# A two-layer centroid convolution block: patch transfers one per slot, the norm six slots earlier, an image's last steps split between ScalarE and VectorE

## The chip, the cores and the metric

The kernel runs on one core of one Trainium2 chip. The metric is the device time of one execution in microseconds; the time before is a median of three runs. A core has TensorE (PE in the profile; its weight loads are PEld), VectorE (DVE), ScalarE (ACT), GpSimd (POOL) and SyncE (SP). Each engine works through its own instructions in the order written and waits on semaphores for the others. Transfers are issued from the queues of ScalarE, GpSimd and SyncE.

## The reference, cut to what matters

The block works on 16 images of 256 channels and 28 x 28 pixels. It is `x + relu(SE(BN2(amm2(relu(BN1(amm1(gn(x))))))) + gn(x))`, where `gn` is a group norm with 32 groups, SE a squeeze-and-excite gate, and `amm` a 3 x 3 convolution replaced by soft look-ups:

```python
patches = jax.lax.conv_general_dilated_patches(x, (3, 3), (stride, stride), 'SAME')
p = patches.reshape(B, C, s, Ho * Wo).transpose(0, 3, 1, 2)
d = jnp.sum(p * p, axis=-1)[..., None] - 2.0 * jnp.einsum('bncs,cks->bnck', p, centroids) + ...
attn = jax.nn.softmax(-d, axis=-1)
lut = jnp.einsum('cks,cso->cko', centroids, w_sub)
out = jnp.einsum('bnck,cko->bno', attn, lut)
```

For each pixel and channel the nine neighbours are compared with 16 centroids, the softmax over them mixes the centroids into a nine-vector again, and these vectors of all channels are multiplied with the 2304 x 256 weights.

## The kernel before, in words

**Tiles.** Channels go through the kernel three to a row tile of 32 partitions, and eight row tiles make a group: 11 groups cover the 256 channels. The 784 pixels are cut in two parts of 384 and 400. An image in one layer is a *stage*: 2 parts x 11 groups = 22 *slots*. The stages of the two layers alternate: layer 0 of image 0, layer 0 of image 1, layer 1 of image 0, layer 0 of image 2, layer 1 of image 1 and so on, 32 stages in all.

**A group.** `patches` (L531) loads the group's patch rows from a DRAM buffer (`pat`) by GpSimd's queue, into `pt` for a pair of groups and into `pm` for a single one. `logits` (L547) does sixteen small matmuls into two PSUM pairs; ScalarE takes the exponential (`b_exp`, L619); `b_num` (L623) does sixteen more into another pair; VectorE transposes that (`nt`, L641), takes the reciprocal of the sums (`rc`, L645) and keeps its largest and smallest value in a column of `ext` (L648, L649); GpSimd scales (`c_scale`, L662, L668); ScalarE fills in columns (`c_fill`, L678); VectorE transposes back (`q`, L689); and `c_look` (L694) accumulates the large matmuls (L700) over nine groups. All PSUM work but these accumulators goes through three pairs used in turn, so PE waits when a pair's reader is late.

**Maxed groups.** In layer 1, groups 0, 3 and 6 get their maxima subtracted first: an extra `logits`, two transposes (`z`, L572), two maxima on VectorE (`mx`, `a_max`, L580), and a way through DRAM on SyncE's queue, two transfers out (`dm`, L598) and two in (`pm`, L606).

**Preparing a stage.** Layer 0 needs the norm of the next image: `load_x` (GpSimd's queue), `gn_stats` and `gn_apply` on VectorE, `gn_mean` and `gn_var` with a tiny matmul each. Then `shift` copies the image into two side buffers (ScalarE), and `to_pat` (L465) writes image and sides to `pat` in 15 transfers on ScalarE's queue, 7056 KB in all.

**The end of an image.** `close` (L801) plans `se_hidden` and `se_gate` (PE, ScalarE, then VectorE from L505 to L510), four `finish` steps (the gate on ScalarE, L519, then two instructions on VectorE, L520 and L521) and `store`. It falls into slots 6 to 12 of the stage that follows.

**What sets the order.** `Plan` (L733) is a table: `at(slot, pos, ...)` puts a step into a slot and a position in it, and `emit` writes all steps in that order. So a step's slot and position decide what it stands behind on its engine. In the table of before the 15 transfers stand two to a slot at position 8 (three where `near`, for the first and the last image's layer 1), the norm in slots 1 to 4 and its transfers in slots 6 to 13 of the layer-1 stage ahead of the stage that needs them, layer 1's transfers in slots 2 to 9 of the layer-0 stage ahead. A maxed group's first logits stand five slots ahead of its second.

Of the kernel before, what the change touches and what calls it, by code (L numbers as in the profile page):

```python
# [8 lines left out]
F32 = mybir.dt.float32  # L9
# [70 lines left out]
def kernel(  # L80
# [148 lines left out]
    NSTAT = B * len(PXT) * (2 * NG - len(MAXED))  # L229
    ext = const.tile([P, 2, NSTAT], F32, name="ext")  # L230
# [173 lines left out]
    mpool = ctx.enter_context(tc.tile_pool(name="mpool", bufs=3))  # L404
# [59 lines left out]

    def to_pat(l, i, pat):  # L465
        dx, (j, k, p0, n, rt) = (1, 0, 2)[i // len(PIECES)], PIECES[i % len(PIECES)]
        base, step = PROW[j * 3 + dx]
        v = (ims[l] if dx == 1 else sides[dx])[p0 : p0 + n, k]
        nc.scalar.dma_start(  # L469
            view(pat, (32 * rt + base) * HW, [[32 * HW, n], [step * HW, 3], [1, HW]]),  # L470
            bass.AP(v.tensor, v.offset, [list(v.ap[0]), [W, 3], [1, HW]]),
        )
# [20 lines left out]
    def se_gate(b):  # L493
        hid = se[b]
# [6 lines left out]
        for k in range(NB):  # L501
            nc.scalar.activation(
                gt[:, k : k + 1], ps[:, k : k + 1], AF.Exp, bias=nb2_sb[:, k : k + 1], scale=-1.0
            )
        nc.vector.tensor_scalar_add(gt, gt, 1.0)  # L505
# [6 lines left out]

    def finish(b, k, i):

        gt, nb = se[b]
        v = slice(i * (HW // 2), (i + 1) * (HW // 2))
        y, xt = ys[b][0][:, k, v], xs[b][:, k, v]
        _, rstd = nrm[b]
        nc.scalar.activation(y, y, AF.Identity, bias=nb[:, k : k + 1], scale=gt[:, k : k + 1])  # L519
# [56 lines left out]
    def a_max(u, gi):  # L576
        nb = blocks(u)
        for v, z in enumerate(u.pop(("z", gi))):
            a = 4 * gi + 2 * v
            nc.vector.tensor_reduce(  # L580
                u["mx"][:, a : a + 2].rearrange("p i (c b) -> p i b c", c=2)[:, :, :nb],
                z[:, : 64 * nb].rearrange("p (i b c k) -> p i b c k", i=2, c=2, k=K),
                axis=AX.X, op=ALU.max,
            )
# [52 lines left out]
    def b_turn(u, gi):  # L637
# [8 lines left out]
        if u["col"][gi] is not None:  # L646
            col = u["col"][gi]
# [4 lines left out]
    qxs = {}  # L652

# [79 lines left out]
    class Plan:  # L733
# [19 lines left out]
        def stage(self, l, b, pat, s0, units, maxed, cols):  # L753
            at = self.at
            for pi, px in enumerate(PXT):
                n0 = n = s0 + pi * NG
                of = {}
                for gs in units:
# [3 lines left out]
                        "groups": gs, "maxed": mx, "col": [None if mx else cols.pop() for _ in gs],  # L762
# [204 lines left out]
```

## Time and profile before

| | us |
|---|---|
| median of 3 runs | 3373.09 |
| lowest, highest | 3366.08, 3379.22 |
| the profiled execution | 3380.56 |
| its span in the trace | 3379.1 |
| PE busy, share of the span | 92% |
| VectorE busy, share of the span | 72% |
| ScalarE, GpSimd busy | 44%, 39% |

The times of instructions come from the one profiled execution, 7.5 us above the median. A row of the windows view gives a stretch's start and end, then for PE, PEld, DVE, ACT and POOL the busy time and the number of instructions, then the granted TensorE clock (1.00 is full speed), the busy share of the DMA engines and GB/s. A row of the waits reads "engine and line that waited <- who ended the wait: us in total, times, longest". A row of the timeline gives start, duration, engine, line, operation and count, with the idle time ahead and who ended it in brackets; ACTq and SPq are transfers being issued, during which the engine counts as idle. A grouped row gives count, busy time and mean ns of one, then the idle time ahead of the group.

### The profile page before, as it was taken

What the parts mean: (1) busy time and instruction counts of PE and PEld (TensorE: products, weight loads), DVE (VectorE), ACT (ScalarE), POOL (GpSimd) and SP (SyncE); (2) the same over time, 40 slices, a digit from 0 to 9 for tenths busy, and PEclk for the clock granted to TensorE, in tenths of its full rate; (3) what the DMA queues carried; (4) which work ended last, traced back from release to release, by engine and by line L of the source; (5) the groups of instructions that cost most, each with busy time, mean ns of one, the idle gap of its engine ahead of it and who ended that gap; (6) DMA issues with size and microseconds to landing.
All of it is one profiled execution on the core that took longest, in us unless ns stands there. A gap on an engine that the chain in (4) does not pass through costs nothing.

```text
span 3379.1 us, 72223 instructions
## 1 busy us (share of the span) xinstructions
PE 3123.8 (92%) x29086; PEld 1220.5 (36%) x29086; DVE 2441.5 (72%) x4132; ACT 1477.0 (44%) x2443; POOL 1305.4 (39%) x1347
## 2 busy tenths in 40 slices
PE   4589999999999999999999999999999999999997
PEld 3133333333333333333333333333333333333333
DVE  2255868777686877868687686868778687776786
ACT  1234354444444444444444444444444444444343
POOL 1133334343443434344343434433343444334332
PEclk8689999999999999999999999999999999999998
DMA  7555554555656355555645656454565545456532
GB/s 232 121 173 177 181 190 133 186 191 166 207 167 196 122 185 194 189 196 162 195 139 177 202 180 200 154 185 156 174 211 181 187 156 191 161 169 202 174 108 68
DMA packets 232373, 586.02 MB, mean 173 GB/s; under 512 B 76238, under 2 KB 89182, under 8 KB 232030
## 3 DMA queue, kind: packets, MB, share of 16 engines
q0 software_dynamic: 76544, 321.16, 29.6%
q10 hardware_dynamic: 82666, 238.70, 21.2%
q1 hardware_dynamic: 72820, 21.45, 2.9%
q8 instruction: 232, 3.80, 0.5%
q14 instruction: 111, 0.91, 0.1%
HBM read 328.23 MB, written 257.82 MB: 173 GB/s over the span
## 4 chain that ended last, share of the span: by engine, by line
PE 42%; DVE 31%; DMA 12%; POOL 6%; issue 4%; ACT 3%; ACTq 2%; SPq 0%; POOLq 0%; DVEq 0%
PE acc L700 21%; PE pair L553 10%; DVE nt L641 9%; DVE q L689 8%; PE pair L629 8%; POOL nt L662 6%; DVE rc L645 5%; DMA pm<-dm 3%; DVE mx L580 3%; DMA xt<-in_x 2%; ACTq L469 2%; DVE z L572 2%; DMA dm<-mt 2%; DVE y L520 1%; ACT y L519 1%
## 5 line engine op out<-in xcount | busy, mean ns | idle before, releaser
L700 PE MATMUL acc<-q,ws 128*128 128x384 f32 (+1 forms) x4608 | 1740.5, 513 | 0.0
L619 ACT ACTIVATE e<-pair 128x768 f32<-128x768 f32 (+1 forms) x1408 | 1084.4, 821 | 1382.0 <-PE pair L553 1138.8
L662 POOL TENSOR_TENSOR nt<-nt,rc 128x648 f32<-128x648 f32 (+1 forms) x576 | 775.0, 1345 | 1599.7 <-DVE rc L645 1470.7
L700 PEld LDWEIGHTS acc<-q,ws 128*128 128x128 f32 x4608 | 814.8, 190 | 920.0 <-issue 483.1
L689 DVE STREAM_TRANSPOSE q<-nt 128x768 f32<-128x768 f32 (+1 forms) x576 | 575.6, 999 | 431.1 <-POOL nt L662 381.5
L641 DVE STREAM_TRANSPOSE nt<-pair 128x768 f32<-128x768 f32 (+1 forms) x704 | 690.7, 981 | 220.3 <-PE pair L629 217.9
L629 PE MATMUL pair<-e,cw 64*32 64x384 f32 (+1 forms) x11264 | 666.3, 509 | 147.1 <-ACT e L619 78.4
L553 PE MATMUL pair<-pt,wd 31*64 31x384 f32 (+1 forms) x9216 | 566.9, 519 | 2.7 <-DVE z L572 1.5
L645 DVE RECIPROCAL rc<-nt 128x72 f32<-128x72 f32 (+1 forms) x704 | 438.4, 623 | 24.2
L629 PEld LDWEIGHTS pair<-e,cw 64*32 64x32 f32 x11264 | 141.6, 105 | 544.5 <-ACT e L619 265.8
L678 ACT COPY nt<-qx 128x120 f32<-128x120 f32 (+1 forms) x576 | 184.3, 320 | 330.7 <-DVE rc L645 327.6
L668 POOL TENSOR_TENSOR qx<-nt,rc 128x324 f32<-128x324 f32 (+3 forms) x256 | 169.5, 700 | 384.5 <-DVE rc L645 384.2
L553 PEld LDWEIGHTS pair<-pt,wd 31*64 31x64 f32 x9216 | 148.2, 131 | 397.4 <-issue 320.2
L538 POOL DMA_DIRECT2D pt<-pat x288 | 228.2, 793 | 39.7 <-DMA pat<-side 37.9
L553 PE MATMUL pair<-pm,wd 31*64 31x384 f32 (+1 forms) x3584 | 219.9, 527 | 8.8 <-DVE nt L641 4.5
L572 DVE STREAM_TRANSPOSE z<-pair 128x768 f32<-128x768 f32 (+1 forms) x192 | 184.0, 995 | 59.1 <-PE pair L553 59.0
L580 DVE TENSOR_REDUCE mx<-z 128x48 f32<-128x768 f32 (+1 forms) x192 | 177.8, 969 | 0.0
L648 DVE TENSOR_REDUCE ext<-rc 128x1 f32<-128x72 f32 (+1 forms) x608 | 140.5, 231 | 20.9
L649 DVE TENSOR_REDUCE ext<-rc 128x1 f32<-128x72 f32 (+1 forms) x608 | 134.1, 221 | 0.0
L553 PEld LDWEIGHTS pair<-pm,wd 31*64 31x64 f32 x3584 | 55.5, 132 | 148.1 <-issue 83.3
L520 DVE SCALAR_TENSOR_TENSOR y<-xt,gn_rstd,y 128x392 f32<-128x392 f32 x64 | 47.9, 749 | 75.5 <-ACT y L519 75.5
L538 POOL DMA_DIRECT2D pm<-pat x128 | 93.0, 726 | 0.0
(102 smaller groups left out, 663.7 us busy)
## 6 DMA issues: line engine op xcount, KB each, us to landing
pt<-pat POOLq DMA_DIRECT2D x144, 800.0 KB, 8.1
pt<-pat POOLq DMA_DIRECT2D x144, 768.0 KB, 5.0
pat<-side ACTq DMA_DIRECT2D x128, 771.8 KB
pat<-im ACTq DMA_DIRECT2D x64, 771.8 KB
pat<-side ACTq DMA_DIRECT2D x64, 404.2 KB
pm<-pat POOLq DMA_DIRECT2D x64, 400.0 KB, 4.8
xt<-in_x POOLq DMA_DIRECT2D x32, 784.0 KB, 6.6
pm<-pat POOLq DMA_DIRECT2D x64, 384.0 KB, 5.3
```

The lines of the kernel that those rows point to most:

```text
L538: nc.gpsimd.dma_start(pt[:, : 2 * len(gs), :n], view(u["pat"], 2 * gs[0] * P * HW + px, [[HW, P], [P * HW, 2 * len(gs)], [1, n]]),)
L553: nc.tensor.matmul(ps[i // 2][64 * h : 64 * h + 64, i % 2, :n], lhsT=wd[l][32 * i : 32 * i + rows, 2 * g + h, :], rhs=u["pt"][32 * i : 32 ...
L572: nc.vector.transpose(z[:, : 64 * nb].rearrange("p (i m) -> p i m", i=2), ps[:, :, : 32 * nb])
L580: nc.vector.tensor_reduce(u["mx"][:, a : a + 2].rearrange("p i (c b) -> p i b c", c=2)[:, :, :nb], z[:, : 64 * nb].rearrange("p (i b c k) ...
L619: nc.scalar.activation(e[:, :, :n], ps[:, :, :n], AF.Exp, scale=2.0)
L629: nc.tensor.matmul(ps[32 * i : 32 * i + 32, h, :n], lhsT=cw[l][64 * h : 64 * h + 64, g, i, :], rhs=es[i // 2][64 * h : 64 * h + 64, i % 2, ...
L641: nc.vector.transpose(t[:, : 2 * nb].rearrange("p (h b) r -> p h (b r)", h=2), u.pop(("nm", gi))[:, :, : 32 * nb])
L645: nc.vector.reciprocal(rc[:, : 2 * nb], t[:, : 2 * nb, SUM : SUM + 3])
L662: nc.gpsimd.tensor_tensor(v, v, rc[:, : 2 * nb].unsqueeze(3).to_broadcast([P, 2 * nb, 3, 9]), ALU.mult)
L678: nc.scalar.copy(u["nt", gi][0][:, : 2 * nb].rearrange("p (h b) r -> p h b r", h=2)[:, :, :, SUM:], bass.AP(w.tensor, w.offset, [list(w.ap ...
L689: nc.vector.transpose(q[:, : 64 * nb], t[:, : 2 * nb].rearrange("p b r -> p (b r)"))
L700: nc.tensor.matmul(accs[key][:, :n], lhsT=ws[l][:, 2 * g + h, o * P : (o + 1) * P], rhs=u["q", gi][:, 32 * nb * h : 32 * nb * h + n], star ...
```

## The change

It has five parts.

- *Transfers*: the 15 transfers become 12 steps (the last two small pieces of a column shift go together), one step per slot, two where `near`.
- *Norm*: from image 2 on, the load, the norm and its transfers stand six slots earlier, one more between load and statistics: the load in slot 15, the norm in slots 17 to 20 of the layer-0 stage, the transfers in slots 0 to 11 of the layer-1 stage. Layer 1's transfers stand in slots 1 to 12.
- *Maxed groups*: first logits six slots ahead instead of five, and the two maxima one slot apart; the way through DRAM stays where it was. `mpool` has four buffers instead of three.
- *Last steps*: the VectorE part of `se_gate` becomes `se_scale`, a slot later; `finish` loses the gate to a step `gate` at position 8, with its VectorE part one slot behind at position 9; the store is two slots later.
- *Extremes*: in place of one `ext` with 608 columns reduced at the end, two small ones used by stages in turn, and `watch`, four small VectorE instructions per stage.

```diff
-    mpool = ctx.enter_context(tc.tile_pool(name="mpool", bufs=3))
+    mpool = ctx.enter_context(tc.tile_pool(name="mpool", bufs=4))
...
+    STEPS = [(dx, ps) for dx in (1, 0, 2) for ps in ((0,), (1,), (2,), (3, 4))]
...
+    def gate(b, k, i):
+
+        gt, nb = se[b]
+        y = ys[b][0][half(k, i)]
+        nc.scalar.activation(y, y, AF.Identity, bias=nb[:, k : k + 1], scale=gt[:, k : k + 1])
...
+    def watch(ext):
+        for i, op in enumerate((ALU.max, ALU.min)):
+            t = small.tile([P, 1], F32, name="ext_t")
+            nc.vector.tensor_reduce(t, ext[:, i], axis=AX.X, op=op)
+            nc.vector.tensor_tensor(worst[:, i : i + 1], worst[:, i : i + 1], t, op)
...
+            if ext is not None:
+                at(s0 + NS + 1, 9, watch, ext)
...
-                            at(s - self.lb, 8, a_max, u, gi)
+                            at(s - self.lb, 8, a_max, u, gi, 0)
+                            at(s - self.lb + 1, 8, a_max, u, gi, 1)
...
-            for i in range(3 * len(PIECES)):
-                self.at(t + 1 + (i // 3 if near else i // 2), 8, to_pat, l, i, pat)
+            for i in range(len(STEPS)):
+                self.at(t + 1 + (i // 2 if near else i), 8, to_pat, l, i, pat)
...
             self.at(te + 2, 9, se_gate, b)
+            self.at(te + 3, 9, se_scale, b)
             for k in range(NB):
                 for i in range(2):
-                    self.at(te + 3 + 2 * k + i, 9, finish, b, k, i)
-            self.at(te + 7, 9, store, b, ob)
+                    self.at(te + 4 + 2 * k + i, 8, gate, b, k, i)
+                    self.at(te + 5 + 2 * k + i, 9, finish, b, k, i)
+            self.at(te + 9, 9, store, b, ob)
...
-    plan = Plan(4, 5)
+    plan = Plan(4, 6)
...
         if l == 0 and b >= 1:
-            plan.at(t - NS, 9, load_x, b, x[b])
-            plan.norm(b, t - NS + 1)
-            plan.prep(0, pat_of(0, b), t - NS + 5, False)
+            t0 = t - NS + (1 if b == 1 else -6)
+            plan.at(t0 - 1, 9, load_x, b, x[b])
+            plan.norm(b, t0 + 1)
+            plan.prep(0, pat_of(0, b), t0 + 5, False)
         if l == 1:
             near = b in (0, B - 1)
-            plan.prep(1, pat_of(1, b), t - NS + (LC + 1 if near else 1), near)
+            plan.prep(1, pat_of(1, b), t - NS + (LC + 1 if near else 0), near)
```

Three places show what this does to the order. First ScalarE in a layer-1 stage, slots 10 to 12. `e` is the exponential of one PSUM pair, the rows named DMA are patch transfers, and the names in brackets are the semaphores that a row waits on; DMAHW0 to DMAHW7 belong to the transfers of ScalarE and SyncE. Before:

```order
L469 DMA pat_82<-side_130 84x3x784 [waits DMAHW0_49]
L469 DMA pat_82<-side_130 4x3x784 [waits DMAHW1_49]
L619 ACTIVATE e<-pair_81 128x800 [waits DVE_49,PE_49,Activation_49]
L619 ACTIVATE e<-pair_79 128x800 [waits DVE_49,PE_49]
L678 COPY nt<-qx 128x24x5 [waits DVE_49,Pool_49]
L469 DMA pat_82<-side_131 84x3x784 [waits DMAHW4_49]
L469 DMA pat_82<-side_131 44x3x784 [waits DMAHW7_49]
L619 ACTIVATE e<-pair_81 128x800 [waits PE_49,Activation_49]
L619 ACTIVATE e<-pair_79 128x800 [waits PE_49,Activation_49]
L469 DMA pat_82<-side_131 40x3x784 [waits DMAHW0_49]
L469 DMA pat_82<-side_131 84x3x784 [waits DMAHW1_49]
```

Now, slots 8 to 10 of the same stage:

```order
L474 DMA pat_82<-side_131 84x3x784 [waits DMAHW2_49]
L632 ACTIVATE e<-pair_79 128x2x384 [waits PE_49,Activation_49]
L632 ACTIVATE e<-pair_80 128x2x384 [waits PE_49,Activation_49]
L697 COPY nt<-qx 128x24x5 [waits DVE_49,Pool_49]
L474 DMA pat_82<-side_131 44x3x784 [waits DMAHW3_49]
L632 ACTIVATE e<-pair_81 128x2x384 [waits DVE_49,PE_49,Activation_49]
L632 ACTIVATE e<-pair_79 128x2x384 [waits DVE_49,PE_49]
...
L474 DMA pat_82<-side_131 40x3x784 [waits DMAHW4_49]
```

A pair of transfers stood between two slots' exponentials; now there is one, and the stage's transfers end two slots earlier.

Second ScalarE in a layer-0 stage, from slot 7 on, where an image's last steps begin. `se_gt` is the exponential of the gate, `y` the gated output. Before:

```order
L469 DMA pat_83<-side_131 84x3x784
L469 DMA pat_83<-side_131 44x3x784
L502 ACTIVATE se_gt<-pair_79,nb_sb 128x1 x2
L619 ACTIVATE e<-pair_81 128x2x384
L619 ACTIVATE e<-pair_79 128x2x384
L678 COPY nt<-qx 128x24x5
L469 DMA pat_83<-side_131 40x3x784
L469 DMA pat_83<-side_131 84x3x784
L519 ACTIVATE y<-y,se_nb,se_gt 128x392
```

Now:

```order
L507 ACTIVATE se_gt<-pair_79,nb_sb 128x1 x2
L632 ACTIVATE e<-pair_81 128x2x384
L632 ACTIVATE e<-pair_79 128x2x384
L697 COPY nt<-qx 128x24x5
L474 DMA pat_83<-side_130 84x3x784
L474 DMA pat_83<-side_130 4x3x784
...
L529 ACTIVATE y<-y,se_nb,se_gt 128x392
L474 DMA pat_83<-side_131 84x3x784
```

The gate stood behind two transfers of its slot; it now stands a slot later, ahead of that slot's one; the rows left out ahead of it are another slot's two exponentials and its copy, which repeat the first slot's.

Third VectorE around the norm's small steps: `gn_gm` and `gn_dv` are the means, `z` and `mx` belong to a maxed group. Before, in slots 2 and 3 of a layer-1 stage:

```order
L429 COPY gn_gm<-pair_80 128x4
L431 TENSOR_TENSOR gn_dv<-gn_mv,gn_gm 128x2
L432 TENSOR_TENSOR gn_dv<-gn_dv 128x2
L572 STREAM_TRANSPOSE z<-pair_81 128x768
L572 STREAM_TRANSPOSE z<-pair_79 128x768
L641 STREAM_TRANSPOSE nt<-pair_80 128x768
L645 RECIPROCAL rc<-nt 128x72
L580 TENSOR_REDUCE mx_147<-z 128x2x12x2 x2
L589 STREAM_TRANSPOSE mt<-mx_147 128x128
L440 TENSOR_TENSOR gn_var<-gn_gm,pair_80 128x2
```

Now, in slots 17 and 18 of a layer-0 stage (the statistics' two rows come twice):

```order
L422 BN_STATS gn_st<-xt 128x6 x2
L423 BN_AGGR gn_mv<-gn_st 128x2
L587 STREAM_TRANSPOSE z<-pair_79 128x768
L587 STREAM_TRANSPOSE z<-pair_80 128x768
L708 STREAM_TRANSPOSE q<-nt 128x832
L654 STREAM_TRANSPOSE nt<-pair_81 128x832
L658 RECIPROCAL rc<-nt 128x78
L661 TENSOR_REDUCE ext_151<-rc 128x1
L662 TENSOR_REDUCE ext_151<-rc 128x1
L593 TENSOR_REDUCE mx_147<-z 128x2x12x2
L431 COPY gn_gm<-pair_81 128x4
```

The statistics now stand directly ahead of a maxed group's two transposes, and one maximum instead of two stands in the slot.

More of the change, by code (lines that the diff above doesn't have):

```diff
@@ L227 @@
         nc.vector.memset(t, 0.0)
[L229 to L230 removed]
+    exts = [const.tile([P, 2, len(PXT) * NG], F32, name=f"ext{i}") for i in range(2)]
+    worst = const.tile([P, 2], F32, name="worst")
+    nc.vector.memset(worst, 1.0)
     nb2_sb = const.tile([P, NB], F32, name="nb2_sb")
@@ L761, in stage @@
                         "l": l, "b": b, "pi": pi, "px": px, "pat": pat, "key": (l, b, pi),
-                        "groups": gs, "maxed": mx, "col": [None if mx else cols.pop() for _ in gs],
+                        "groups": gs, "maxed": mx, "ext": ext,
                     }
```

72 lines of the change are left out of this document (36 added, 36 removed).

## The prediction

> **What bounds the kernel now.** I read the page first, then windows over equal stretches of the program, then the waits, then the timeline where windows differ.
>
> ```profile
> span 3379.1 us, 72223 instructions
> PE 3123.8 (92%) x29086; PEld 1220.5 (36%) x29086; DVE 2441.5 (72%) x4132; ACT 1477.0 (44%) x2443; POOL 1305.4 (39%) x1347
> ```
>
> TensorE is busy 92% of the span, so the question is what one slot of the plan costs when nothing disturbs it. I cut each stage at the exponentials (two L619 per slot). Slots 13 to 17 of the 14 layer-0 stages from the fourth stage on carry only the steady work; one of the 14 windows, and their sum:
>
> ```profile
> core 0: us, PE busy (x) PEld busy (x) DVE busy (x) ACT busy (x) POOL busy (x), PEclk, DMA share, GB/s
> 1709.20:1729.20 20.00, 20.00 (x193) 7.78 (x194) 13.24 (x24) 9.92 (x17) 10.63 (x12) 1.00 0.42 143
> sum 279.20, PE 279.20 PEld 108.18 DVE 184.13 ACT 138.94 POOL 148.37; mean PE 19.94 PEld 7.73 DVE 13.15 ACT 9.92 POOL 10.60
> ```
>
> PE is busy all of it: 19.94 us for five slots, 3.99 us each. That is the pace to reach. Three stretches miss it. First, slots 8 to 12 of the same stages, where an image's last steps stand (two of 14 rows, and the sum):
>
> ```profile
> 1287.20:1312.20 25.00, 20.74 (x199) 8.39 (x196) 19.60 (x34) 11.32 (x18) 7.88 (x8) 1.00 0.64 221
> 1683.60:1709.20 25.60, 22.16 (x195) 9.02 (x196) 19.55 (x34) 11.44 (x18) 7.87 (x8) 0.93 0.64 217
> sum 362.60, PE 306.98 PEld 121.49 DVE 281.51 ACT 161.05 POOL 110.58; mean PE 21.93 PEld 8.68 DVE 20.11 ACT 11.50 POOL 7.90
> ```
>
> That is 362.60/14 = 25.90 us for five slots. Second, slots 9 to 12 of 13 layer-1 stages, under the patch transfers (two rows, and the sum):
>
> ```profile
> 1591.50:1612.50 21.00, 18.68 (x171) 6.88 (x172) 16.05 (x26) 6.87 (x11) 6.91 (x7) 1.00 0.83 278
> 2186.80:2210.00 23.20, 20.29 (x171) 7.17 (x172) 16.77 (x27) 6.91 (x12) 6.90 (x7) 0.93 0.79 265
> sum 276.70, PE 247.51 PEld 90.65 DVE 211.98 ACT 90.01 POOL 89.99; mean PE 19.04 PEld 6.97 DVE 16.31 ACT 6.92 POOL 6.92
> ```
>
> 276.70/13 = 21.28 us for four slots. Third, from slot 18 of a layer-0 stage to slot 4 of the layer-1 stage behind it, nine slots with the norm (sum of 13):
>
> ```profile
> sum 562.10, PE 541.17 PEld 206.66 DVE 509.48 ACT 230.86 POOL 235.25; mean PE 41.63 PEld 15.90 DVE 39.19 ACT 17.76 POOL 18.10
> ```
>
> 562.10/13 = 43.24 us, of which VectorE works 39.19. The waits name who is late in these stretches:
>
> ```profile
> ACT e L619 <- DMA pat<-side: 93.8, 18, 8.0
> DVE y L520 <- ACT y L519: 75.5, 59, 3.9
> ACT e L619 <- DMA pat<-im: 75.4, 24, 3.8
> PE pair L629 <- DVE nt L641: 68.3, 95, 3.0
> DVE se_gt L505 <- ACT se_gt L502: 47.4, 16, 6.9
> DVE gn_st L420 <- DMA xt<-in_x: 23.3, 15, 7.8
> ```
>
> **Part A, an image's last steps split by engine.** One such stretch, ScalarE, VectorE and TensorE in turn:
>
> ```profile
> 1685.79 2.93 ACTq L469 DMA_DIRECT2D pat<-side  x2
> 1688.77 0.71 ACT L519 ACTIVATE y<-y,se_nb,se_gt 128x392 f32<-128x392 f32 x1 [2.69 <-issue]
> ...
> 1689.51 0.62 DVE L520 SCALAR_TENSOR_TENSOR y<-xt,gn_rstd,y 128x392 f32<-128x392 f32 x1 [3.44 <-ACT y L519]
> ...
> 1694.29 0.73 DVE L520 SCALAR_TENSOR_TENSOR y<-xt,gn_rstd,y 128x392 f32<-128x392 f32 x1 [0.76 <-ACT y L519]
> ...
> 1699.06 0.86 DVE L520 SCALAR_TENSOR_TENSOR y<-xt,gn_rstd,y 128x392 f32<-128x392 f32 x1 [0.65 <-ACT y L519]
> ...
> 1692.64 0.88 PE L629 MATMUL pair<-e,cw 64*32 64x384 f32 x16 [2.54 <-DVE nt L641]
> ...
> 1694.38 3.75 PE L700 MATMUL acc<-q,ws 128*128 128x384 f32 x6
> ...
> 1699.73 2.20 PE L700 MATMUL acc<-q,ws 128*128 128x384 f32 x6
> ```
>
> Two transfers hold ScalarE's queue for 2.93 us; the gate (L519) waits behind them, VectorE waits 3.44 us for the gate, the transpose queued behind it on VectorE is late, and PE stands 2.54 us. The change puts the gate ahead of the slot's transfer and the VectorE half one slot later; the add and reciprocal (L505) also go one slot behind their exponentials. Both waits (75.5 and 47.4 us in all) lose their cause. What is late next is VectorE itself: from 1694.29 to 1699.06 a slot takes it 4.77 us, 0.65 of it idle, so 4.12 of work, against 20.74/5 = 4.15 for PE (the full-clock row). They tie, so I leave 1.0 us of the stretch's loss standing: 25.90 - 20.74 - 1.0 = 4.2 us, times 15 (the 14 stages and image 14's steps in the last stage; the last image's run with nothing beside them) = 63 us. Bounds: 2.5 us if only the first gate's 3.44 us wait goes and about 1 us of it was slack (38), and 5.2 with nothing left (78).
>
> The clock is part of that. In 7 of the 14 windows the granted clock reads 0.93 or 0.94, as in the row at 1683.60; the six matmuls at 1694.38, right behind the 2.54 us gap, took 3.75 us and the same six later 2.20. At 0.065 x 25.8 us in 7 windows this is 12 us, which I let go with the gaps. [...]
>
> **Part B, one patch transfer per slot.** Layer 1, slots 10 to 12, SyncE, PE and ScalarE:
>
> ```profile
> 1599.26 2.43 SPq L606 DMA_DIRECT2D pm<-dm  x2
> ...
> 1605.10 2.85 PE L700 MATMUL acc<-q,ws 128*128 128x384 f32 x8
> ...
> 1608.21 0.76 ACTq L469 DMA_DIRECT2D pat<-side  x2
> 1609.08 0.84 ACT L619 ACTIVATE e<-pair 128x800 f32<-128x800 f32 x1 [5.49 <-DMA pat<-side]
> ...
> 1609.96 1.61 PE L629 MATMUL pair<-e,cw 64*32 64x400 f32 x16 [2.02 <-ACT e L619]
> 1611.50 0.93 PE L553 MATMUL pair<-pm,wd 31*64 31x400 f32 x16
> ```
>
> The instruction order shows each transfer waiting on one of eight semaphores that ScalarE's and SyncE's transfers use in turn; it is issued when the user eight transfers back has landed. With two a slot and SyncE's four per maxed group between, that one is about 2.5 slots old. At 1608.21 ScalarE has waited for it, the next exponential 5.49 us, and PE 2.02 us. Spread over twelve steps (fifteen transfers still, nine slots with one and three with two), the eighth back is three to four slots old, 12 us or more. The stretch's floor is four slots and one maxed group's logits, 4 x 3.99 + 0.93 = 16.9 us, so at most 21.28 - 16.9 = 4.4 us can go; PE's visible idle is 21.28 - 19.04 = 2.2. I take 3.6, nearer to the upper end because PE's busy time itself is stretched there (1.61 us for sixteen matmuls that steadily take about 0.9). Fourteen images (2 to 15): 50 us, bounds 31 and 62. The issues cost ScalarE the same as before, only in more slots.
>
> **Part C, the norm six slots ahead, the two maxima apart, the extremes kept per stage.**
>
> ```profile
> L420 DVE BATCH_NORM_STATS2 gn_st<-xt 128x6 f32<-128x392 f32 x64 | 32.3, 546 | 23.3 <-DMA xt<-in_x 23.3
> L421 DVE BATCH_NORM_AGGREGATE gn_mv<-gn_st 128x2 f32<-128x12 f32 x32 | 6.7, 209 | 1.1
> L449 DVE TENSOR_SCALAR im<-xt,gn_gm,gn_rstd 128x784 f32<-128x784 f32 x32 | 34.6, 1122 | 1.2 <-POOL gn_rstd L238 1.2
> L648 DVE TENSOR_REDUCE ext<-rc 128x1 f32<-128x78 f32 x304 | 71.2, 234 | 10.4
> L431 DVE TENSOR_TENSOR gn_dv<-gn_mv,gn_gm 128x2 f32<-128x2 f32 x16 | 5.1, 321 | 0.5
> L440 DVE TENSOR_TENSOR gn_var<-gn_gm,pair 128x2 f32<-128x2 f32 x16 | 2.0, 122 | 0.7 <-PE pair L438 0.7
> ```
>
> The norm is 4 x 0.546 + 2 x 0.209 = 2.6 us of statistics, 2.2 of applying and under 1 of small work, 5.7 us on VectorE. It leaves slots 1 to 4 of layer 1 for slots 17 to 20 of layer 0: the same busy stretch, one slot longer, with the same three maxed groups in it. The image is loaded two slots ahead, so the wait for it (23.3/15 = 1.55 us) goes. New are four small reductions per stage, 2 x 0.234 and two between 0.122 and 0.321: 0.7 to 1.1 us, free in a layer-0 stage (VectorE works 13.15 of 19.94 us there), paid behind it. Net: zero. Bounds: 1.55 x 14 = 22 gained; 2.6 x 14 = 36 lost, if the statistics stand in front of the transposes that PE's buffer pairs wait for.
>
> **Ends.** Image 15's transfers go two instead of three a slot, the last reductions shrink, the first stage's last transfer now stands right ahead of the patches that read it, and the last store but one comes two slots nearer to the write of its buffer. An estimate of 8 us either way, from the landings below; zero in the sum.
>
> **Sum.** 63 + 50 = 113. The profiled execution took 3380.56 us, 7.5 above the median of the runs, 3373.09; 3380.6 - 113 = 3267.6, and against the median 3260.
>
> **Rivals.** *The transfers keep ScalarE waiting.* For: DMA share 0.83 at 1591.50 against 0.42 in the quiet window; bytes and the eight semaphores are unchanged. Against: 0.42 is what is left over the rest of the stage. B is then zero: 3373 - 63 = 3310. [...]
>
> *VectorE gives it back.* Slots 17 to 20 hold 4 x 13.15/5 = 10.5, 5.7 of norm and about 4.1 of a maxed group, 20.3 us against PE's 4 x 3.99 + 0.93 = 16.9. Were PE to wait 8 us for that in 14 images, 112 us return: 3372, no change. Against: the old place had the same plus 1.55 of waiting.
>
> *GpSimd stands on the last transfer: slower.*
>
> ```profile
> pt<-pat POOLq DMA_DIRECT2D x144, 800.0 KB, 8.1
> pm<-pat POOLq DMA_DIRECT2D x64, 384.0 KB, 5.3
> ```
>
> The last transfer of a layer-1 image now stands in slot 12, and the first maxed group's patches, which read it, in slot 14 of GpSimd's queue, ahead of the scalings that the transposes need. Two slots are 8.0 us, and GpSimd has 3.99 - 10.60/5 = 1.9 to spare. To end 0.5% slower than 3373 (about what a measurement of this kernel can tell from no change, 17 us), 15 images must each lose (113 + 17)/15 = 8.7 us: a landing of 18.6 us or more. Transfers of this size land in a median of 8.1 us; against it.
>
> **Numbers.** Forecast 0.68, transfers 0.12 (also faster), VectorE 0.11 (same), GpSimd 0.09 (slower): faster 0.80. With all upper bounds 78 + 62 + 22 + 8 = 170, 3203; with all lower ones 38 + 31 - 36 - 8 = 25, 3348. The range 3205 to 3350 holds the forecast and the first rival.
>
> **What would show it.** Right: slots 8 to 12 of layer 0 near 21.7 us, VectorE's wait for the gate (L535 on L529) near zero, the exponential's (L632) for patch transfers below 40 us, layer 1's slots 9 to 12 near 17.7, the clock at 1.00 in most windows. Wrong: PE waiting for VectorE's transposes in slots 17 to 21, GpSimd idle ahead of the maxed group's patches, or the exponentials waiting for transfers in twelve slots.

## The result, and the profile after

The changed kernel takes 3273.39 us (median of 4 runs, 3269.2 to 3281.93) against 3376.15 for the kernel before on the same chip: 102.8 us less, a ratio of 0.9704 [0.9674, 0.9733]. The forecast was 3260, 113 us less; the range held the time. The profiled execution of after took 3269.2 us.

The page of after, span and engines:

```profile
span 3267.5 us, 72362 instructions
PE 3106.2 (95%) x29086; PEld 1214.2 (37%) x29086; DVE 2527.0 (77%) x4261; ACT 1475.2 (45%) x2443; POOL 1313.0 (40%) x1347
```

The same matmuls now fill 95% of a span that is 111.6 us shorter. The stretches of the prediction, cut in the same way at the exponentials (now L632), give as sums over 14 layer-0 stages for slots 8 to 12 and for slots 13 to 17, then over 13 stretches from layer-0 slot 18 to layer-1 slot 4:

```profile
sum 286.60, PE 285.04 PEld 114.20 DVE 263.49 ACT 154.19 POOL 110.54; mean PE 20.36 PEld 8.16 DVE 18.82 ACT 11.01 POOL 7.90
...
sum 333.80, PE 306.47 PEld 116.09 DVE 274.63 ACT 141.98 POOL 176.96; mean PE 21.89 PEld 8.29 DVE 19.62 ACT 10.14 POOL 12.64
...
sum 547.20, PE 545.38 PEld 206.28 DVE 497.87 ACT 261.20 POOL 216.42; mean PE 41.95 PEld 15.87 DVE 38.30 ACT 20.09 POOL 16.65
```

Slots 8 to 12 fell from 25.90 to 286.60/14 = 20.47 us, 1.2 us below the forecast's 21.7. Slots 13 to 17, which were full of PE at 19.94, rose to 23.84. Part of that is work that moved: a maxed group's first logits now stand in slot 17, no longer in slot 18. So the two stretches are better read as one, from slot 13 to slot 4 of the next stage, which holds the same 591 matmuls in both kernels: first before, then after, 13 stretches each.

```profile
sum 821.40, PE 800.47 PEld 307.16 DVE 680.49 ACT 359.90 POOL 373.05; mean PE 61.57 PEld 23.63 DVE 52.34 ACT 27.68 POOL 28.70
```

```profile
sum 858.80, PE 830.01 PEld 314.06 DVE 754.49 ACT 393.05 POOL 381.44; mean PE 63.85 PEld 24.16 DVE 58.04 ACT 30.23 POOL 29.34
```

That is 63.18 us before and 66.06 after: 2.9 us a stage were given back here. Layer 1's slots 5 to 13, with three maxed groups in both kernels, went the other way, again before and then after:

```profile
sum 576.10, PE 546.91 PEld 205.34 DVE 443.81 ACT 230.42 POOL 210.29; mean PE 42.07 PEld 15.80 DVE 34.14 ACT 17.72 POOL 16.18
```

```profile
sum 527.80, PE 527.80 PEld 199.69 DVE 442.92 ACT 204.76 POOL 209.60; mean PE 40.60 PEld 15.36 DVE 34.07 ACT 15.75 POOL 16.12
```

From 44.32 to 40.60 us, with PE busy all of it. Slots 9 to 12 alone, which the prediction had near 17.7 us, take 247.80/13 = 19.06: with the first logits a slot earlier they hold 188 matmuls, not 171, and PE is busy all of them. The waits of after that answer to those of before, and two of GpSimd's:

```profile
DVE q L708 <- POOL nt L681: 367.6, 364, 5.4
POOL pt L553 <- DMA pat<-side: 43.2, 2, 38.1
PE pair L568 <- DVE z L587: 27.6, 20, 3.0
POOL nt L681 <- DMA pat<-side: 26.1, 12, 2.2
ACT e L632 <- DMA pat<-side: 22.8, 5, 7.6
DVE gn_st L422 <- DMA xt<-in_x: 11.3, 5, 8.1
DVE se_gt L514 <- ACT se_gt L507: 6.8, 1, 6.8
ACT e L632 <- DMA pat<-im: 3.4, 1, 3.4
DVE y L535 <- ACT y L529: 0.8, 1, 0.8
```

VectorE's wait for the gate fell from 75.5 to 0.8 us, the exponential's for patch transfers from 93.8 + 75.4 to 22.8 + 3.4. New among the long ones is PE's wait for the transpose `z` (L587), and 23.6 of its 27.6 us have one place. Layer-0 slot 17, VectorE and then PE:

```profile
1669.29 1.04 DVE L422 BATCH_NORM_STATS2 gn_st<-xt 128x6 f32<-128x392 f32 x2 [0.29 <-DMA xt<-in_x]
...
1671.50 0.21 DVE L423 BATCH_NORM_AGGREGATE gn_mv<-gn_st 128x2 f32<-128x12 f32 x1
1671.63 1.79 DVE L587 STREAM_TRANSPOSE z<-pair 128x768 f32<-128x768 f32 x2
...
1669.79 0.90 PE L642 MATMUL pair<-e,cw 64*32 64x400 f32 x16
1672.61 1.76 PE L568 MATMUL pair<-pt,wd 31*64 31x400 f32 x16 [1.92 <-DVE z L587]
1674.31 3.01 PE L719 MATMUL acc<-q,ws 128*128 128x400 f32 x4
```

The statistics hold VectorE from 1669.29 to 1671.6, `z` follows them, and PE stands 1.92 us for the pair that `z` empties. Such a gap, 1.53 to 2.96 us, is in slot 17 of all 13 layer-0 stages from the fourth to the twenty-eighth.

### The profile page after: what moved, and what is told of

It reads as the page before. It is cut to its first block, busy times and chain, and to the rows that moved or that the text cites. A ratio compares the mean times of both kernels' runs of the same rounds, so it can differ in the third digit from the quotient of the medians.

```text
span 3267.5 us, 72362 instructions
## 1 busy us (share of the span) xinstructions
PE 3106.2 (95%) x29086; PEld 1214.2 (37%) x29086; DVE 2527.0 (77%) x4261; ACT 1475.2 (45%) x2443; POOL 1313.0 (40%) x1347
## 4 chain that ended last, share of the span: by engine, by line
PE 73%; DVE 17%; DMA 5%; POOL 3%; issue 2%; ACT 1%; ACTq 0%; SPq 0%; POOLq 0%; DVEq 0%
PE acc L719 39%; PE pair L568 18%; PE pair L642 14%; DVE nt L654 4%; DVE q L708 3%; DVE rc L658 3%; POOL nt L681 3%; DVE y L535 2%; DMA xt<-in_x 1%; DMA pat<-side 1%; DVE gn_st L422 1%; DVE z L587 1%; DVE y L536 1%; DMA dm<-mt 1%; PE pair L336 1%
## 5 line engine op out<-in xcount | busy, mean ns | idle before, releaser
L632 ACT ACTIVATE e<-pair 128x768 f32<-128x768 f32 (+1 forms) x1408 | 1087.4, 822 | 1450.0 <-PE pair L568 1373.6
L708 DVE STREAM_TRANSPOSE q<-nt 128x768 f32<-128x768 f32 (+1 forms) x576 | 578.5, 1004 | 413.9 <-POOL nt L681 367.6
L642 PE MATMUL pair<-e,cw 64*32 64x384 f32 (+1 forms) x11264 | 641.8, 507 | 52.1 <-ACT e L632 43.4
L687 POOL TENSOR_TENSOR qx<-nt,rc 128x324 f32<-128x324 f32 (+3 forms) x256 | 178.9, 737 | 392.0 <-DVE rc L658 392.0
L642 PEld LDWEIGHTS pair<-e,cw 64*32 64x32 f32 x11264 | 131.1, 105 | 422.3 <-ACT e L632 200.7
L568 PE MATMUL pair<-pm,wd 31*64 31x384 f32 (+1 forms) x3584 | 237.9, 513 | 4.4 <-DVE z L587 3.7
L587 DVE STREAM_TRANSPOSE z<-pair 128x768 f32<-128x768 f32 (+1 forms) x192 | 182.4, 987 | 67.3 <-PE pair L568 67.3
L593 DVE TENSOR_REDUCE mx<-z 128x48 f32<-128x768 f32 (+1 forms) x192 | 186.1, 969 | 0.0
L535 DVE SCALAR_TENSOR_TENSOR y<-xt,gn_rstd,y 128x392 f32<-128x392 f32 x64 | 76.9, 1202 | 0.8 <-ACT y L529 0.8
```

What stands on the lines that cost most here:

```text
L568: nc.tensor.matmul(ps[i // 2][64 * h : 64 * h + 64, i % 2, :n], lhsT=wd[l][32 * i : 32 * i + rows, 2 * g + h, :], rhs=u["pt"][32 * i : 32 ...
L587: nc.vector.transpose(z[:, : 64 * nb].rearrange("p (i m) -> p i m", i=2), ps[:, :, : 32 * nb])
L593: nc.vector.tensor_reduce(u["mx"][:, a : a + 2].rearrange("p i (c b) -> p i b c", c=2)[:, :, :nb], u["z", gi].pop(0)[:, : 64 * nb].rearran ...
L632: nc.scalar.activation(e[:, :, :n], ps[:, :, :n], AF.Exp, scale=2.0)
L642: nc.tensor.matmul(ps[32 * i : 32 * i + 32, h, :n], lhsT=cw[l][64 * h : 64 * h + 64, g, i, :], rhs=es[i // 2][64 * h : 64 * h + 64, i % 2, ...
L708: nc.vector.transpose(q[:, : 64 * nb], t[:, : 2 * nb].rearrange("p b r -> p (b r)"))
```

## Experiments

### The two halves taken apart

Part A (the last steps split by engine) and part B (the transfers spread) were put on the kernel before one at a time. The runs were made on several chips, on which the kernel before took medians of 3374.03 to 3379.18 us, so each run is given against the kernel before on its own chip, and a difference of a few us between two runs says little. A alone, *before_close*:

```diff
...
+            self.at(te + 3, 9, se_scale, b)
             for k in range(NB):
                 for i in range(2):
-                    self.at(te + 3 + 2 * k + i, 9, finish, b, k, i)
-            self.at(te + 7, 9, store, b, ob)
+                    self.at(te + 4 + 2 * k + i, 8, gate, b, k, i)
+                    self.at(te + 5 + 2 * k + i, 9, finish, b, k, i)
+            self.at(te + 9, 9, store, b, ob)
```

> The kernel before with only the last steps of an image split by engine (the gate ahead of the slot's transfer, the VectorE half a slot later); transfers two per slot and the norm as before. The prediction's part A taken alone: 63 us less (38 to 78), 3298 to 3338 against 3376. Rival, theory L (the chain of VectorE's reciprocal, GpSimd's scaling, the product on VectorE and the next slot's copy takes 4.23 us a slot against TensorE's 3.99, so that what slots 8 to 12 save is lost again in slots 13 to 17): slots 8 to 17 of a layer-0 stage were 45.9 us before and are 44.3 after, so 1.6 x 14 = 22 us less, 3345 to 3365, with slots 13 to 17 above 21.5 us.

3316.28 us (3314.05 to 3331.61) against 3375.57, a ratio of 0.9836 [0.9801, 0.9871]: 59 us less. The prediction's 63 held; theory L, as a statement on this edit, fell: slots 13 to 17 take 283.60/14 = 20.26 us, not above 21.5. Its waits:

```profile
ACT e L626 <- DMA pat<-im: 86.5, 27, 3.7
ACT e L626 <- DMA pat<-side: 79.6, 16, 7.7
...
DVE y L527 <- ACT y L520: 0.8, 1, 0.8
```

VectorE's wait for the gate is gone with the transfers still two a slot, and ScalarE's waits for transfers stand as they were.

B alone, *before_spread*:

```diff
-                self.at(t + 1 + (i // 3 if near else i // 2), 8, to_pat, l, i, pat)
+                n = 4 * (i // len(PIECES)) + min(i % len(PIECES), 3)
+                self.at(t + 1 + (n // 2 if near else n), 8, to_pat, l, i, pat)
```

> The kernel before with only the transfers spread to one per slot; they stand in slots 6 to 17 of layer 1, the last one right ahead of the patches in slot 18. The prediction's part B taken alone: 50 us less (31 to 62), 3314 to 3345; by the run with two per slot 60 or more less, 3305 to 3316, with VectorE's wait for the gate also falling from 75.5 us to below 50. The GpSimd rival (patches wait on the last transfer, scalings behind them late): 3390 or more, GpSimd waiting over 8 us per stage ahead of the patches.

3274.10 us (3273.31 to 3278.38) against 3375.57, 0.9702 [0.9673, 0.9730]: 101 us less, twice the prediction's 50 and as much as the whole change. Its sums for layer-0 slots 8 to 12 and layer-1 slots 5 to 13:

```profile
sum 324.20, PE 287.19 PEld 115.27 DVE 265.22 ACT 163.38 POOL 110.54; mean PE 20.51 PEld 8.23 DVE 18.94 ACT 11.67 POOL 7.90
...
sum 532.50, PE 528.37 PEld 201.68 DVE 443.36 ACT 232.85 POOL 209.98; mean PE 40.64 PEld 15.51 DVE 34.10 ACT 17.91 POOL 16.15
```

Layer 1 gave 44.32 - 532.50/13 = 3.4 us a stage, which is the prediction's 3.6. But slots 8 to 12 of layer 0, where the prediction booked nothing for B, gave 25.90 - 324.20/14 = 2.7 us a stage, 38 us in all: with one transfer in a slot the gate stands behind one, not two. Its waits:

```profile
POOL pt L538 <- DMA pat<-side: 58.9, 14, 38.9
DVE y L520 <- ACT y L519: 53.9, 59, 1.5
...
ACT e L619 <- DMA pat<-im: 43.7, 12, 3.7
...
ACT e L619 <- DMA pat<-side: 7.7, 3, 3.1
```

The longest wait for a gate is now 1.5 us, not 3.9. I had expected the total below 50 us; it is 53.9. The exponentials still wait 43.7 + 7.7 = 51 us for patch transfers, against 169 before. GpSimd does stand on a transfer ahead of the patches, but for (58.9 - 38.9)/13 = 1.5 us at a time (the longest wait, 38.9 us, is in the kernel before as well, with 37.9), not for the 8 of the rival.

The other side, on the changed kernel. A taken out, *undo_close*:

```diff
...
-            self.at(te + 3, 9, se_scale, b)
+            self.at(te + 2, 9, se_scale, b)
             for k in range(NB):
                 for i in range(2):
-                    self.at(te + 4 + 2 * k + i, 8, gate, b, k, i)
-                    self.at(te + 5 + 2 * k + i, 9, finish, b, k, i)
-            self.at(te + 9, 9, store, b, ob)
+                    self.at(te + 3 + 2 * k + i, 9, gate, b, k, i)
+                    self.at(te + 3 + 2 * k + i, 9, finish, b, k, i)
+            self.at(te + 7, 9, store, b, ob)
```

> The changed kernel with the image's last steps as before: gate and VectorE half in one slot, at position 9 behind the patch transfer, the se_gate arithmetic in one slot, the store two slots earlier. Theory of three separate causes: the gate's wait comes back, though behind one transfer instead of two, so slots 8 to 12 of layer 0 rise from 20.5 us to 23 to 26, 15 times: 3273 + 40 to 80 = 3310 to 3350, and VectorE's wait for the gate is 50 us or more. Rival, that the gain came from VectorE's load being moved between stages and ScalarE's queue being free: with one transfer per slot the gate is hardly held, so slots 8 to 12 stay under 21.5 us and the time under 3290.

3278.81 us (3277.2 to 3279.23) against 3376.83, 0.9713 [0.9685, 0.9741]: 5 us above the changed kernel, too little to tell the two apart by their intervals. The time is the rival's, the place is not. Two of its waits:

```profile
DVE y L535 <- ACT y L529: 54.2, 59, 1.6
...
PE pair L568 <- DVE z L587: 16.6, 27, 1.8
```

The gate's wait is back (54.2 us), and slots 8 to 12 take 324.40/14 = 23.17 us, not the rival's 21.5: A still takes 2.7 us a stage out of them when the transfers are spread. But slots 13 to 17 take 311.50/14 = 22.25 us here and 23.84 in after, and PE's longest wait for `z` is 1.8 us and not 3.0. So in the changed kernel most of what A gains in its own slots is given back right behind them.

B taken out, *two_per_slot* (`to_one` writes one of the 15 pieces):

```diff
...
-            for i in range(len(STEPS)):
-                self.at(t + 1 + (i // 2 if near else i), 8, to_pat, l, i, pat)
+            for i in range(3 * len(PIECES)):
+                self.at(t + 1 + (i // 3 if near else i // 2), 8, to_one, l, i, pat)
```

> The changed kernel with the 15 patch transfers two to a slot again (three where near), all else as changed. Theory of three separate causes: ScalarE waits for landings again, about 3.6 us per image in layer 1, and some in layer 0: 3273 + 35 to 65 = 3310 to 3340, the exponential's wait for patch transfers back above 100 us. Rival, that the spacing is hidden because the norm's move took VectorE's load out of layer 1: under 3290, though the exponential still waits for transfers.

3336.53 us (3335.24 to 3338.42), 0.9886 [0.9858, 0.9914]: 63 us above the changed kernel. The exponentials wait for transfers again:

```profile
ACT e L641 <- DMA pat<-side: 70.2, 18, 8.5
ACT e L641 <- DMA dm<-mt: 56.3, 18, 3.9
ACT e L641 <- DMA pm<-dm: 47.0, 9, 6.1
```

`dm` and `pm` are SyncE's transfers of the maxed groups: the semaphore that ScalarE's issue waits on was last used by one of them.

### Both halves, and nothing else

*close_spread* is before_close and before_spread in one: A and B without C.

> The kernel before with the last steps split by engine and the transfers spread, and nothing of part C (norm, maxima and extremes as before). Theory O (the split and the spreading remove the same waits, and part C costs): from the spread-only run at 3274, slots 8 to 17 of a layer-0 stage fall from 43.1 to 40.8 us (20.5 and 20.3, as in the run with the split alone and in the changed kernel), 2.3 x 14 = 32 less, 3235 to 3250; part C then costs 25 to 38 us of the changed kernel. Rival (the split is worth nothing once the transfers are spread, and part C costs nothing): 3266 to 3278.

3247.58 us (3246.28 to 3248.72) against 3374.03, 0.9629 [0.9604, 0.9655]: 126 us less. Theory O held: slots 8 to 17 of a layer-0 stage take (285.90 + 285.20)/14 = 40.8 us. The crossing as a table, us less than the kernel before on the same chip:

| | without C | with C |
|---|---|---|
| A | 59.3 | 40.3 |
| B | 101.5 | 98.0 |
| A and B | 126.5 | 102.8 |

A and B together are 59.3 + 101.5 - 126.5 = 34.3 us short of their sum. Most of this both remove: slots 8 to 12 fall by 25.90 - 297.30/14 = 4.7 us with A alone (before_close), and by 23.16 - 285.90/14 = 2.7 with A on top of B, 27 us less in 14 stages. C costs 19.0 us on A, 3.5 on B and 23.7 on both. That it costs so little on B alone (undo_close) goes with the shorter waits for `z` there; A also moves the VectorE half of the last `finish` step from slot 11 to slot 13. Which of these decides is not settled. For both, the stretch from slot 13 to slot 4 of the next stage shows the cost: the sum of 13 in close_spread,

```profile
sum 828.00, PE 802.77 PEld 308.62 DVE 720.67 ACT 362.79 POOL 381.25; mean PE 61.75 PEld 23.74 DVE 55.44 ACT 27.91 POOL 29.33
```

is 63.69 us against 66.06 in after; 2.37 x 13 = 31 us are lost there, and 7 gained elsewhere.

### What in C costs

The norm one slot earlier and one later, each one number in the changed kernel (*norm_slot16* with -7, *norm_slot18* with -5):

```diff
-            t0 = t - NS + (1 if b == 1 else -6)
+            t0 = t - NS + (1 if b == 1 else -7)
```

> The changed kernel with the norm one slot earlier still, statistics in slot 16 of layer 0, so that a whole slot lies between them and the maxed group's two transposes of slot 18. Theory that PE waits in slot 17 because the 2.4 us of statistics stand directly ahead of those transposes, and that the clock then halves: PE's wait there falls from 1.5 to 3 us to under 0.5, the half-clock periods of these stages go, and 1.5 to 2.7 us per image come back: 3273 - 20 to 38 = 3235 to 3253. Rival, that the stretch is bound by VectorE's sum of work wherever the norm stands: 3268 to 3278.

3280.89 us (3280.37 to 3283.07), 0.9723 [0.9699, 0.9746]; both expectations missed. It is 7.5 us slower, though its interval and that of the changed kernel overlap. The gap only changed its owner:

```profile
PE pair L429 <- DVE nt L654: 35.7, 14, 3.3
```

Now the norm's first matmul (L429), which stands ahead of other work on PE and needs a buffer pair, waits 35.7/14 = 2.5 us in slot 17 for VectorE's `nt`, and the image's load is late as well (VectorE waits 31.1 us for it in 15 times, 11.3 in after).

> The changed kernel with the norm one slot later, statistics in slot 18 of layer 0, behind the maxed group's two transposes instead of ahead of them, and the applying in slot 21, behind the next group's. Theory of the place: PE's wait for the transposes in slot 17 goes; the statistics' 2.4 us now delay the next slot's transpose instead, which has about a slot of slack less what the transposes took, so half of the loss comes back: 3273 - 5 to 30 = 3243 to 3268. Rival, VectorE's sum of work: 3268 to 3278.

3265.95 us (3263.76 to 3270.91), 0.9678 [0.9654, 0.9702]: 7.4 us faster, as the theory of the place had it, again with overlapping intervals. PE's wait for `z` is down to one of 1.4 us; the wait of norm_slot16, L429 for `nt`, is there with 13.8 us in 14 times.

Both maxima in one slot again, and with them the first logits five slots ahead instead of six (the 5 in the last line), *maxes_together*:

```diff
-                            at(s - self.lb + 1, 8, a_max, u, gi, 1)
+                            at(s - self.lb, 8, a_max, u, gi, 1)
...
-                        e = n + len(gs) - self.lb
+                        e = n + len(gs) - 1 - self.lb
...
-    plan = Plan(4, 6)
+    plan = Plan(4, 5)
```

> The changed kernel with both maxima of a maxed group in one slot again (and so the group's reductions all one slot later relative to its logits). If two maxima in two slots are worth what the prediction said, nothing: 3268 to 3280. If the burst of two maxima on VectorE delays the transposes and copies that TensorE waits for: 5 to 15 us slower, 3278 to 3290. If the place relative to the norm's statistics decides: 5 to 15 us faster, 3258 to 3268, with the gap in slot 17 gone.

3283.61 us (3272.84 to 3288.94), 0.9724 [0.9691, 0.9758]. The median speaks for the burst on VectorE, but its runs reach down to the time of the changed kernel; no verdict. The third expectation fell: the gap is still there in 13 stages, a slot later, and it is L429 that waits for `nt` (31.9 us in 14 times, 3.2 at most). So taking back the maxima and the lead alone does not give back what C costs.

### The product behind the next copy

In slots 13 to 17 VectorE goes round a loop that is no part of the change. VectorE and then GpSimd in after:

```profile
1657.49 1.04 DVE L708 STREAM_TRANSPOSE q<-nt 128x832 f32<-128x832 f32 x1 [1.19 <-POOL nt L681]
1658.46 1.01 DVE L654 STREAM_TRANSPOSE nt<-pair 128x832 f32<-128x832 f32 x1
1659.50 0.64 DVE L658 RECIPROCAL rc<-nt 128x78 f32<-128x78 f32 x1
...
1661.71 1.05 DVE L708 STREAM_TRANSPOSE q<-nt 128x832 f32<-128x832 f32 x1 [1.17 <-POOL nt L681]
...
1660.30 1.38 POOL L681 TENSOR_TENSOR nt<-nt,rc 128x702 f32<-128x702 f32 x1 [1.41 <-DVE rc L658]
```

`q` of a slot waits for GpSimd's scaling, GpSimd for VectorE's reciprocal, and on VectorE that reciprocal stands behind the `q` of the slot before. The round takes 1661.71 - 1657.49 = 4.22 us, 1.2 of it idle, against PE's 3.99 us a slot: once late, VectorE cannot catch up while this lasts. The kernel before has the same round (`q` starts at 1715.54 and at 1719.77, 4.23 us apart) in slots that are full of PE at 3.99, so the round alone does not hold PE up within five slots. One number breaks it, *q_behind*:

```diff
-                            at(s + 2, 2, c_turn, u, gi)
+                            at(s + 2, 5, c_turn, u, gi)
```

> The changed kernel with one number altered: the product q moved on VectorE behind the copy and reciprocal of the next slot, so that VectorE no longer stands idle for GpSimd's scaling ahead of that copy. Theory L: VectorE's wait for GpSimd ahead of the product falls from 367.6 us to below 120, slots 13 to 17 of layer 0 from 23.85 to 20 to 21 us, the total to 3215 to 3255. Rival (VectorE is simply full in slots 8 to 21, waits on it are slack): 3266 to 3281, with the idle time only moved to other VectorE instructions.

3226.63 us (3224.33 to 3231.98) against 3375.57, 0.9560 [0.9536, 0.9584]: 47 us below the changed kernel. Its waits, and its sum for slots 13 to 17 of layer 0:

```profile
DVE nt L654 <- PE pair L642: 592.6, 443, 73.1
...
DVE q L708 <- POOL nt L681: 7.9, 2, 7.7
```

```profile
sum 318.60, PE 304.13 PEld 115.08 DVE 254.62 ACT 137.12 POOL 168.06; mean PE 21.72 PEld 8.22 DVE 18.19 ACT 9.79 POOL 12.00
```

VectorE's wait for GpSimd went from 367.6 to 7.9 us, and VectorE now waits for PE, as it should where PE is the bound. The total is where theory L had it; slots 13 to 17 are not, at 318.60/14 = 22.8 us instead of 20 to 21: they hold a maxed group's logits (0.9 us) as well, and what is left of the gap of slot 17 (PE waits 18.3 us for `z` in 15 times).

The same number in close_spread, *close_spread_q*:

> close_spread with the product q moved on VectorE behind the copy and reciprocal of the next slot. If the loop through GpSimd's scaling costs only where the norm crowds VectorE in slots 17 to 20 (theory O: there is no such crowd here ahead of slot 18): 0 to 12 us less than close_spread, 3225 to 3245. If the loop by itself slows every slot (theory L): 30 or more us less than close_spread, below 3215.

3190.41 us (3187.6 to 3197.7) against 3374.03, 0.9459 [0.9433, 0.9485]: 57 us below close_spread. The total is where theory L had it, and VectorE's wait for GpSimd falls from 412.8 to 0.2 us. Its sums for slots 13 to 17 and for the stretch from slot 13 to slot 4:

```profile
sum 279.30, PE 279.30 PEld 108.28 DVE 209.37 ACT 137.15 POOL 148.60; mean PE 19.95 PEld 7.73 DVE 14.95 ACT 9.80 POOL 10.61
...
sum 802.60, PE 796.00 PEld 305.96 DVE 706.32 ACT 355.21 POOL 373.00; mean PE 61.23 PEld 23.54 DVE 54.33 ACT 27.32 POOL 28.69
```

Slots 13 to 17 are full of PE, and the stretch takes 61.74 us, 1.4 less than before. But a loop that slows every slot, as theory L had it, is not what these sums show: against close_spread slots 13 to 17 gave 285.20/14 - 19.95 = 0.4 us, and the nine slots behind them, where the norm and the maxed groups crowd VectorE in this kernel too, 563.10/13 - 543.30/13 = 1.5. In 14 and 13 stages that is 26 of the 57 us; the rest is spread over the other stretches. This is the fastest kernel of the study, 83 us below the changed one and without part C.

*q_behind_norm18* is q_behind with -5 in the norm's line.

> The changed kernel with the product moved behind the next copy and the norm one slot later. The norm's later place was worth 7 us with the product in its old place (3265.95 against 3273.39). If both help apart: 3212 to 3224. If the product's place already frees VectorE in slot 17, so that nothing is left for the norm's place to give: 3224 to 3232.

3252.23 us (3247.91 to 3257.39), 0.9643 [0.9616, 0.9669]: 26 us slower than q_behind, against both expectations. What came out 7 us faster with `q` in its old place hurts here. PE's wait is in a new place: the logits of slot 19 wait for `gn_gm`, the norm's small step on VectorE (17.0 us in 14 times), where q_behind has no such wait, and the granted clock of the whole execution is 0.974 instead of 0.979.

### The norm put back

The last run has the product moved and the norm in its old place, with the maxima and extremes of the change, *norm_back_q*:

```diff
-                            at(s + 2, 2, c_turn, u, gi)
+                            at(s + 2, 5, c_turn, u, gi)
...
-            t0 = t - NS + (1 if b == 1 else -6)
+            t0 = t - NS + (1 if b == 1 else 0)
```

> The changed kernel with the product moved behind the next copy and the norm put back to slots 1 to 4 of layer 1, maxima apart and extremes per stage as in the change. Against the run with only the product moved (3226.6) it differs by the norm's place alone, against the split and spread kernel with the product moved (3190.4) by the maxima and extremes alone. If the norm's place is what part C costs: 3183 to 3200. If the maxima apart or the extremes cost it: 3215 to 3235. In between, shared.

3226.89 us (3222.99 to 3235.11) against 3379.18, 0.9546 [0.9518, 0.9574]. The second expectation held. Between these two places of the norm the difference is 3226.89 - 3226.63 = 0.3 us, nothing (3.4 against the kernel before on each chip). What is left of C, the maxed groups' new order and the extremes, with the image's load and layer 1's transfers one slot earlier, costs 3226.89 - 3190.41 = 36 us (31 against the kernel before on each chip). Its layer-1 slot 1, VectorE and then PE:

```profile
1488.15 1.03 DVE L422 BATCH_NORM_STATS2 gn_st<-xt 128x6 f32<-128x392 f32 x2
...
1490.48 1.79 DVE L587 STREAM_TRANSPOSE z<-pair 128x768 f32<-128x768 f32 x2
...
1491.46 1.74 PE L568 MATMUL pair<-pm,wd 31*64 31x384 f32 x16 [1.29 <-DVE z L587]
```

The maxed groups' first logits, six slots ahead instead of five, have moved from slot 2 into slot 1, where the statistics are: the picture of slot 17 again. PE waits here in each of 13 layer-1 stages, 1.29 to 2.01 us, 19 us in all, and the stretch from slot 13 to slot 4 takes 824.20/13 = 63.40 us against 61.74. So neither of the two places frees C of its cost, and at both `z` stands right behind the statistics. That this meeting is the cause is argued, not shown: norm_slot18 and q_behind_norm18 have the statistics behind `z`, and the first is 7 us faster, the second 26 slower. How much of the 36 us is the meeting, and how much the extra reductions, which stand right ahead of the statistics here, and the later second maximum, no run separates.

## Why the prediction was right in its number and where its steps failed

**Part A, 63 us: right alone, not in the sum.** The edit alone measured 59, through the wait that was named: the gate behind the transfers. On top of B it is worth 126.5 - 101.5 = 25 us, because B takes one of the two transfers away that the 3.44 us of the quoted timeline waited for; on top of B and C it is worth 5, no clear difference. The prediction costed A against the kernel before and added B as if that were untouched; 34 us of the sum are not there, 27 of them counted twice in slots 8 to 12. That VectorE ties with PE came out for these slots (20.47 us, PE busy 20.36), so the 1.0 us left standing was too much; what the working left out is the slots behind them.

**Part B, 50 us: the step that failed.** Its layer-1 size was right (3.4 us a stage against 3.6). What was missing is layer 0: the spacing was costed only where ScalarE's exponentials waited for a transfer's semaphore, and not where an issue simply stood ahead of the gate. Between the two traces, from exponential to exponential, 44 us went from the 13 layer-1 stages, 40 from the 14 layer-0 stages, 18 from the first three stages and 5 from the last but one: 106 of span with rounding, against an upper bound of 62.

**Part C, net zero: wrong, inside its bounds.** It costs 24 us on A and B (and 3.5 on B alone). The bound on the losing side named the mechanism, statistics in front of the transposes that PE's pairs wait for, and 2.6 us x 14 = 36 as its price; the forecast took zero because "the same busy stretch" has the same work. PE's work is the same, 591 matmuls; the order in slot 17 is not. The wait for the load did fall from 23.3 to 11.3 us. Which piece of C the 24 us hang on stays open: the norm a slot earlier, a slot later or (with `q` moved) at its old place, and the maxima put back, each left most of the cost.

**The clock, 12 us of A: right for these slots.** All 14 stretches of slots 8 to 12 read 1.00 in after, where 7 read 0.93 or 0.94. So the reduced clock went with the gaps there, as the prediction had it. But it came back behind nine of the 13 gaps of slot 17, and the granted clock of the whole profiled execution is 0.974 before and 0.976 after; more is said below.

**The rivals.** Transfers that keep ScalarE waiting: no, 26 us are left of 169. The same bytes, spaced, cost ScalarE's exponentials 143 us less of waiting. VectorE giving it back: in part, 24 of 126. GpSimd standing on the last transfer: little, its scaling waited 26.1 us in 12 times, 2.2 at most, where the rival needed 8.7 per image, and the large patch loads land as fast as before:

```profile
pt<-pat POOLq DMA_DIRECT2D x144, 800.0 KB, 7.4
```

**The sum.** 59.3 + 101.5 - 34.3 - 23.7 = 102.8. The forecast of 113 was near this by luck: a B that was 52 us too small, a shortfall of 34 where A and B overlap and an unpriced C of 24 nearly cancelled. Of the signs that would show it wrong, one appeared and was right: PE waiting for VectorE's transposes in slot 17. Of those that would show it right, one failed: layer 1's slots 9 to 12 took 19.06 us, not 17.7, in part because the floor of the working had one maxed group's logits in them (0.93 us) where the new order has two.

## What to carry to other kernels

Two edits that shorten the same stretch have to be costed one on top of the other: ask of the second what it still finds. A transfer's issue delayed what stood behind it on its queue also where the profile shows it waiting for nothing (the 2.93 us ahead of the gate), so look for every such place when issues are spaced; here layer 0's was worth nearly as much as layer 1's. Before moving a step into a stretch with room, look at which instruction it will stand directly in front of, and who waits for that one; and look for rounds between engines whose time is just above the slot of the bound, since one position in the order may break them (47 and 57 us here).

## What the runs showed of the hardware

In after, the granted clock halves behind nine of the 13 gaps of slot 17. Around the gap of slot 17 that is quoted above, and then the 5.1 us from the end of two other such gaps, of 1.54 and 1.53 us:

```profile
1672.60:1674.30 1.70, 1.69 (x16) 0.41 (x16) 1.70 (x3) 0.67 (x1) 0.00 (x0) 1.00 0.90 351
1674.30:1677.10 2.80, 2.80 (x8) 1.48 (x5) 2.73 (x6) 1.30 (x3) 0.96 (x1) 0.51 0.02 6
...
707.10:712.20 5.10, 5.09 (x30) 2.21 (x38) 4.56 (x7) 2.00 (x3) 1.56 (x2) 0.67 0.37 141
...
2056.40:2061.50 5.10, 5.10 (x51) 2.03 (x54) 4.96 (x11) 1.98 (x3) 1.60 (x2) 1.00 0.36 136
```

Here the half clock (0.51) sets in 1674.37 - 1672.61 = 1.8 us after PE is back at work; behind the other eight it is 0.1 to 2.4 us. Of the 13 gaps, 1.53 to 2.96 us, nine were followed by a reduced clock in the 5.1 us after them (0.51 to 0.73) and four were not (1.00), and gaps of 1.53 and 1.54 us are in both sets: the length of the gap alone doesn't decide. The place in time does go with it. The trace's record of the clock has the reduced periods of these stages start at 517.25, 708.39, 899.54, 1094.10, 1285.25, 1479.81, 1674.37, 1865.51 and 2824.66 us; each lasts 3.41 us, or 6.83 in the three from 899.54, 1285.25 and 1479.81. Any two of the nine starts are a whole multiple of 3.4133 us apart to within 0.03 us (708.39 - 517.25 = 191.14, and 56 x 3.4133 = 191.14); of all lengths from 1 to 20 us only this one fits them so. Counted from such marks, the five gaps of 1.53 to 1.56 us that a reduced clock followed begin 0.0 to 0.9 us behind one, and the four that none followed begin 1.6 to 1.7 us behind one. What keeps the starts to these steps, no run shows.

What the reduced clock costs is less than it seems. By these rows (1 - clock) x 5.1 us adds to 16 us over the nine. But the two stages with the gaps of 1.54 and 1.53 us compare directly, from slot 13 to slot 4 of the next stage:

```profile
684.50:750.10 65.60, 63.80 (x591) 24.15 (x591) 57.95 (x100) 30.14 (x47) 29.31 (x32) 0.97 0.55 172
...
2033.70:2098.80 65.10, 62.86 (x591) 23.76 (x592) 57.91 (x100) 30.40 (x48) 29.37 (x32) 1.00 0.55 172
```

The stage with the reduced clock takes 0.5 us more, not (1 - 0.67) x 5.1 = 1.7, and the one at full clock still takes 1.4 us more than the 63.69 of close_spread. So the clock is at most part of what C costs.
